# A two-layer graph kernel: the first layer's rows stored in sorted order by SyncE and gathered by the second layer

## The chip, the cores and the metric

The kernel runs on one core of one Trainium2 chip. The metric is the device time of one launch in microseconds (us). Engines are named as the profile names them: PE (TensorE, matmuls; PEld are its weight loads), DVE (VectorE), ACT (ScalarE), POOL (GpSimd) and SP (SyncE, which only issues transfers here).

## What is computed

Sixteen graphs (batches) of 1024 nodes with 64 features are taken through two layers. `adj` is a symmetric 0/1 matrix with the diagonal set.

```python
# layer 0: thin out the neighbours, take weighted quantiles over them per feature, then an MLP
nb      = adj without the diagonal;  m = nb.sum(-1);  rank = cumsum(nb) - 1
skip    = where(m > 10, (m + 1) // 2, 1)
removed = nb & (skip > 1) & ((rank + 1) % skip == 0)        # then symmetrised
valid   = adj with removed and removed.T taken out
agg     = 0.25*q(0.25) + 0.5*q(0.5) + 0.25*q(0.75)          # interpolated quantiles over valid neighbours
y       = relu((x + agg) @ W1 + b1) @ W2 + b2
x1      = layernorm(x + y * nodemask)
# layer 1: messages over the full adjacency
msg     = adj @ x1
d       = tanh(concat(x1, msg) @ W1' + b1') @ W2' + b2'
out     = layernorm(x1 + d)
```

## The kernel before

**Sorting by degree.** For each batch `list_batch` loads the adjacency in eight tiles `a` of 128 rows, makes the neighbour mask `nb` (L623, L626), finds the removed neighbours with matmuls, and counts each node's degree. A counting sort over degrees gives each node its place `at_i` (L685 to L708). Each mask row, with the node's record `mine` (number, degree, the base of the batch's rows in x, nodemask; the constant is set by a GpSimd memset at L681) and its features, is then scattered by GpSimd to its place in the DRAM tensor `order` (L712). From then on, nodes with a similar number of neighbours stand together.

**Groups and chunks.** The sixteen batches form five groups of 2, 4, 4, 4 and 2. The sorted tiles of a group are cut into nine or ten chunks (`CHUNKS`), each with a min/max network of a fixed number of slots, from 40 down to 10. There are 48 chunks. In a chunk by DVE a partition tile mixes rows of all the group's batches; in a chunk by PE (`ChunkByPE`) each tile is of one batch.

**One chunk.** `fetch_lists` loads mask rows (`row`, L806) or features (`x_n`, L931). `fill` of a plain chunk makes neighbour indices with MAX8 (L825 to L831, into `off`, `idx`, with `g.base` added) and gathers neighbours' features slot by slot with GpSimd's indirect DMA (L846, 1012 in all); `fill` of a PE chunk does it with one-hot matmuls (L982, L990). `select` runs the network on DVE (L875), weighs the chosen places (L897, L899), runs the MLP (p_h, p_y) and the layer norm (L550 to L558). At the end of `select` each tile of `y` is scattered by GpSimd to its nodes' rows of the DRAM tensor `g.x1` (L916), so that `g.x1` is in node order. The index of that scatter, `ids`, and the degrees, base and mask of a group in sorted order come from `srt`, which `weigh_group` loads from `order` (L739, L741) before it works out the quantile weights (L744 to L774).

**Second layer.** `messages(g, b)` loads the batch's x1 rows into `x1_n` (L1018; the profile calls it `x_n<-x`; one buffer). Then, eight times, it loads 128 rows of `adj` (L1024), transposes them on PE (L1029), transposes x1 (p_x, L1035), multiplies (p_msg, L1039), and runs the MLP (p_z, tanh L1045, p_d L1048). DVE adds the bias out of p_d into `d` at each of the eight (L1049); p_d has one PSUM buffer, which it shares with p_y. At the end come the residual (L1051), the layer norm and the store (L1053).

**The order of the work.** Each of these is a Python generator. The loop at the end goes through the 48 chunks. Beside the `select` of chunk s it advances, in 24 shares, the `fill` of chunks s+1 and s+2, the `prepare` of the next group (`coming`) and the `finish_group` of the group before (`going`). `prepare` is drained three chunks ahead of its group's first one (`LEAD`). The Tile framework then orders each engine's queue from dependences and its own costs, so an engine's queue isn't exactly in program order. Each engine runs its queue in that order.

Of the kernel before, what the change touches and what calls it, by code (L numbers as in the profile page):

```python
# [9 lines left out]
F32 = mybir.dt.float32  # L10
# [18 lines left out]
INFO = 4  # L29
# [387 lines left out]
def kernel(  # L417
# [37 lines left out]
    off_diag = const.tile([P, P], BF16, name="off_diag")  # L455
    nc.vector.tensor_scalar(off_diag, ident, -1.0, 1.0, op0=ALU.mult, op1=ALU.add)
# [5 lines left out]
    nc.vector.tensor_copy(off_diag_f, off_diag)  # L462
# [22 lines left out]
    zero = const.tile([P, BINS], F32, name="zero")  # L485
    nc.vector.memset(zero, 0.0)
    number = const.tile([P, B * NT], F32, name="number")
    nc.gpsimd.iota(number, pattern=[[P, B * NT]], base=0, channel_multiplier=1,
                   allow_small_or_imprecise_dtypes=True)
# [112 lines left out]
    class Group:  # L602
# [3 lines left out]
        def __init__(self, b0, count):  # L606
            self.b0, self.count, self.tiles, self.run = b0, count, count * NT, P // count
            self.order = [hbm.tile([N, ROW // 2], I32, name=f"order{b0 + i}") for i in range(count)]
            self.x1 = hbm.tile([count * N, C], F32, name=f"x1_{b0}")
            self.parts = []  # L610

    def list_batch(g, b):
# [68 lines left out]
        nc.gpsimd.memset(mine[:, :, 2], float((b + 1) * N))  # L681
        nc.scalar.copy(mine[:, :, 0], number[:, b * NT:(b + 1) * NT])
        nc.scalar.copy(mine[:, :, 3], mask[:, b * NT:(b + 1) * NT])
        deg = mine[:, :, 1]
# [11 lines left out]
        nc.vector.tensor_tensor_scan(base[:, 1:], zero, p[:, :BINS], 0.0, op0=ALU.add, op1=ALU.add)  # L696
# [10 lines left out]
        at_i = work.tile([P, NT], I32, name="at_i")  # L707
# [23 lines left out]
    def weigh_group(g):  # L731
# [11 lines left out]
        ids = work.tile([P, max(GROUPS) * NT], I32, name="ids")[:, :n]  # L743
        nc.vector.tensor_scalar(ids, srt[:, :, 0], float(-g.b0 * N), None, op0=ALU.add)  # L744
        g.local = ids
        g.base, g.mask = srt[:, :, 2], srt[:, :, 3]
        deg = srt[:, :, 1]
# [31 lines left out]
        yield  # L779
# [6 lines left out]
    class Chunk:  # L786
# [26 lines left out]
        def fill(self):  # L813

            g, n = self.g, self.n
            caps = CAPS[g.tiles][self.t0:self.t0 + n]
            wide = -(-(self.k - 1) // 8) * 8
            key = work.tile([P, 96], F16, name="key")[:, :n * wide].rearrange("p (t k) -> p t k", k=wide)
            off = work.tile([P, 96], F32, name="off", bufs=1)[:, :n * wide].rearrange("p (t k) -> p t k", k=wide)
            idx = work.tile([P, 96], I32, name="idx")[:, :n * wide].rearrange("p (t k) -> p t k", k=wide)  # L820
            for t in range(n):
                code = nets.tile([P, N], F16, name="code", bufs=1)
                nc.vector.tensor_mul(code, self.rows[t], down)
                for r in range(0, wide, 8):
                    nc.vector.max(key[:, t, r:r + 8], code)  # L825
                    if r + 8 < wide:
                        nc.vector.match_replace(code, key[:, t, r:r + 8], code, 0.0)  # L827
                yield
            nc.vector.tensor_scalar(off, key, 0.5, OOB, op0=ALU.is_lt, op1=ALU.mult)
            nc.vector.tensor_sub(off, off, key)  # L830
            nc.vector.tensor_add(idx, off, bcast(g.base[:, self.t0:self.t0 + n], wide))  # L831
            self.take_slots()
            at = self.net["slots"]
            for i in range(g.count):
                nc.sync.dma_start(
                    self.a[i * g.run:(i + 1) * g.run, at[0]],
                    g.order[i][self.t0 * g.run:(self.t0 + n) * g.run, XCOL // 2:].bitcast(F32).rearrange(
                        "(t p) c -> p t c", p=g.run))
            for k in range(self.net["low"], self.k):
                nc.scalar.copy(flat(self.a[:, at[k]]),  # L840
                               big[:, (self.k - 1 - k) % 2:(self.k - 1 - k) % 2 + 1].to_broadcast([P, n * C]))
            for k in range(1, max(caps)):
                for t in range(n):
                    if k >= caps[t]:
                        continue
                    nc.gpsimd.indirect_dma_start(  # L846
                        out=self.a[:, at[k], t, :], out_offset=None, in_=x_rows,
                        in_offset=bass.IndirectOffsetOnAxis(ap=idx[:, t, k - 1:k], axis=0),
                        bounds_check=B * N - 1, oob_is_err=False)
                yield  # L850
            self.x_s = self.a[:, at[0]]

        def chosen(self, t, first, count):

            bufs = (self.a.rearrange("p k t c -> p k (t c)"), self.b)
            return [bufs[buf][:, at, t * C:(t + 1) * C]
                    for _, buf, at in self.net["places"][first:first + count]]

# [3 lines left out]
        def select(self):  # L862
# [19 lines left out]
            for h in range(0, n, HT):  # L882
# [23 lines left out]
                p_y = ps_m.tile([P, HT, C], F32, name="p_y", tag="y", bufs=1)  # L906
# [8 lines left out]
            for t in range(n):  # L915
                nc.gpsimd.indirect_dma_start(  # L916
                    out=g.x1, out_offset=bass.IndirectOffsetOnAxis(
                        ap=g.local[:, self.t0 + t:self.t0 + t + 1], axis=0),
                    in_=y[:, t, :], in_offset=None)
            yield  # L920

    class ChunkByPE(Chunk):
# [13 lines left out]
        def fill(self):  # L936
# [8 lines left out]
            for q in range(g.count // 2):  # L945

                degs = work.tile([1, 2, P, 1], F32, name="degs", bufs=1)
                for i in range(2):
                    nc.sync.dma_start(degs[:, i], g.order[2 * q + i][at0:at0 + P, N // 2 + 1:N // 2 + 2].bitcast(
                        F32).rearrange("(o p) i -> o p i", o=1))  # L950
# [53 lines left out]

        def chosen(self, t, first, count):
# [8 lines left out]
    def messages(g, b):  # L1014

        x1 = work.tile([P, NT, C], F32, name="x1_n", bufs=1)
        n0 = (b - g.b0) * N
        nc.sync.dma_start(x1, g.x1[n0:n0 + N, :].rearrange("(t p) c -> p t c", p=P))  # L1018
        d = work.tile([P, NT, C], F32, name="d", bufs=1)
        for h in range(NT // QT):  # L1020
# [25 lines left out]
            p_d = ps_m.tile([P, QT, C], F32, name="p_d", tag="y", bufs=1)  # L1046
            for t in range(QT):
                nc.tensor.matmul(p_d[:, t, :], z_t[:, t * P:(t + 1) * P], w2b_s, start=True, stop=True)  # L1048
            nc.vector.tensor_add(d[:, h * QT:(h + 1) * QT], p_d, b2b_r[:, None, :].to_broadcast([P, QT, C]))  # L1049
            yield  # L1050
        nc.vector.tensor_add(d, d, x1)  # L1051
        layer_norm(work, d, d)
        nc.sync.dma_start(out[b].rearrange("(t p) c -> p t c", p=P), d)  # L1053
        yield

    def prepare(g):
        for b in range(g.b0, g.b0 + g.count):
            yield from list_batch(g, b)
        yield from weigh_group(g)
# [28 lines left out]
    def start(i):  # L1088
        groups[i] = Group(starts[i], GROUPS[i])
        return Side(prepare(groups[i]), GROUPS[i] * (3 * NT + 1) + 1)  # L1090
# [6 lines left out]
    for s in range(-LEAD, len(plan)):  # L1097
# [17 lines left out]
        select = None  # L1115
        if s >= 0:
            i = plan[s][0]
            if s and plan[s - 1][0] != i:
# [41 lines left out]
    work = ctx.enter_context(tc.tile_pool(name="work_g", bufs=1))  # L1160
    ones_row = work.tile([P, N], BF16, name="ones_row")
# [189 lines left out]
```

## Time and profile before

| what | value |
|---|---|
| median of 11 runs | 3148.24 us (3133.44 to 3155.26) |
| the profiled execution | 3143.64 us, span 3141.9 us |
| mean granted PE clock | 0.881 |
| busy: PE / DVE / POOL / ACT | 2383.4 / 2392.6 / 1707.5 / 1574.6 us |
| DMA | 264.34 MB, 84 GB/s over the span |
| x1 scatters (L916) | 128, mean 1429 ns, 350.5 us of POOL idle before them |
| slot gathers (L846) | 1012, mean 1339 ns, 728.2 us of POOL idle before them |
| last layer norm of the first layer (L558 on y) | starts at 3041.8 us |

A row of groups is read as: line, engine, operation, output<-inputs, shape, count, then busy us and mean ns of one, then the engine's idle time just before these instructions and what ended most of it. A row of waits is: engine, tile and line that waited, what it waited for, then total us, number of waits and the longest. In a timeline row the first numbers are the start and the duration in us; in brackets stands the idle time before it with what ended it.

### The profile page before, as it was taken

To read this page: it belongs to the slowest core of one execution; us is meant where nothing else is said; L and a number is where in the kernel's file an instruction comes from. 1 tells how busy PE (TensorE), PEld (TensorE's weight loads), DVE (VectorE), ACT (ScalarE), POOL (GpSimd) and SP (SyncE) were. 2 spreads that over 40 slices of the span, in tenths; PEclk is the share of its full clock that TensorE was granted. 3 is DMA by queue.
4 is the path that set the end of the run, shared out by engine and by line. 5 is a ranking of instruction groups with operands and counts; after the bars stand their busy time and mean duration, and the time that the engine had idled before them with its cause. 6 is when DMAs were issued, how large, how long until landed. Compare 5 with 4: busy or idle time off the path is not lost. (4 is left out here: it accounts for less than half of the span.)

```text
span 3141.9 us, 65767 instructions
## 1 busy us (share of the span) xinstructions
PE 2383.4 (76%) x24920; PEld 1890.8 (60%) x25076; DVE 2392.6 (76%) x5580; ACT 1574.6 (50%) x4045; POOL 1707.5 (54%) x1512
## 2 busy tenths in 40 slices
PE   4456876779586888759888998787889385686977
PEld 2244663457475766547767776666667374575755
DVE  3359985579699978869998888976899387676741
ACT  5624655646254546645566557433554253243543
POOL 3164774256677475757564765485465556333400
PEclk9778987889798998889999999888989697898988
DMA  2520433333222323132334243123222221121222
GB/s 96 158 60 17 120 110 99 98 91 99 82 69 67 123 66 109 50 119 69 114 103 129 62 125 90 50 65 107 73 77 71 69 79 47 51 66 54 82 72 79
DMA packets 221333, 264.34 MB, mean 84 GB/s; under 512 B 147443, under 2 KB 148050, under 8 KB 221008
## 3 DMA queue, kind: packets, MB, share of 16 engines
q1 hardware_dynamic: 174288, 189.31, 19.8%
q0 software_dynamic: 46720, 70.74, 7.8%
q8 instruction: 199, 3.26, 0.4%
q14 instruction: 126, 1.03, 0.1%
HBM read 218.20 MB, written 46.40 MB: 84 GB/s over the span
## 5 line engine op out<-in xcount | busy, mean ns | idle before, releaser
L846 POOL DMA_INDIRECT slots_a<-in_x_dram,idx x1012 | 1355.1, 1339 | 728.2 <-issue 266.0
L990 PE MATMUL p_slots<-hot,parts 128*64 128x256 bf16 (+1 forms) x12288 | 695.1, 269 | 141.0 <-DVE hot L982 136.2
L990 PEld LDWEIGHTS <-parts 128*64 128x64 bf16 x12288 | 632.5, 113 | 179.4 <-issue 111.8
L875 DVE TENSOR_TENSOR slots_b<-slots_a 128x256 f32<-128x256 f32 (+14 forms) x582 | 359.3, 633 | 92.7 <-DMA slots_a<-in_x_dram,idx 58.6
L916 POOL DMA_INDIRECT x<-y,ids x128 | 182.9, 1429 | 350.5 <-DVE y L558 210.3
L899 PE MATMUL p_g<-ident,terms 128*64 128x128 f32 x1988 | 281.6, 295 | 62.5 <-ACT terms L897 61.8
L982 DVE TENSOR_SCALAR hot<-val 128x2048 bf16<-128x2048 bf16 x456 | 310.9, 702 | 15.6 <-PE p_slots L990 12.4
L899 PEld LDWEIGHTS p_g<-ident,terms 128*64 128x64 f32 x1988 | 240.5, 149 | 95.2 <-ACT terms L897 77.8
L875 DVE TENSOR_TENSOR slots_a<-slots_b 128x256 f32<-128x256 f32 (+11 forms) x526 | 288.6, 561 | 0.6
L1039 PE MATMUL p_msg<-adj_t,x_n 128*64 128x128 f32 x2048 | 272.1, 286 | 7.9 <-ACT adj_t L1030 4.2
L1039 PEld LDWEIGHTS p_msg<-adj_t,x_n 128*64 128x64 f32 x2048 | 232.9, 143 | 31.3 <-issue 9.8
L630 ACT ACTIVATE gone<-nb 128x512 bf16<-128x512 bf16 x256 | 159.8, 627 | 174.3 <-DVE nb L626 173.1
L1001 ACT COPY slots_a<-p_slots 128x512 f32<-128x512 f32 (+2 forms) x136 | 72.9, 536 | 300.5 <-PE p_slots L990 243.6
L660 PE MATMUL p_rank<-reach,nb_t 128*128 128x128 bf16 (+3 forms) x956 | 177.0, 318 | 58.4 <-ACT nb_t L654 49.0
L1029 PE MATMUL p_adj<-ident,a 128*128 128x128 f32 x1024 | 185.0, 294 | 43.2 <-ACT adj_t L1030 21.6
L662 ACT ACTIVATE gone<-p_rank,s 128x512 bf16<-128x512 f32 x256 | 166.4, 684 | 97.5 <-PE p_rank L660 84.6
L825 DVE MAX8 key<-code 128x8 f16<-128x1024 f16 x170 | 207.9, 1223 | 2.0 <-DVE code L827 0.5
L712 POOL DMA_INDIRECT order<-nb,at_i x128 | 145.8, 1139 | 110.0 <-issue 40.3
L875 DVE TENSOR_TENSOR slots_b<-slots_b 128x256 f32<-128x256 f32 (+11 forms) x310 | 199.3, 643 | 0.4
L660 PEld LDWEIGHTS <-nb_t 128*128 128x128 bf16 x1024 | 96.8, 105 | 164.8 <-ACT nb_t L654 78.7
L1030 ACT COPY adj_t<-p_adj 128x512 f32<-128x512 f32 x256 | 149.2, 583 | 74.0 <-PE p_adj L1029 72.0
L1049 DVE TENSOR_TENSOR d<-p_d,b2b_r 128x64 f32<-128x64 f32 x128 | 28.5, 223 | 204.3 <-PE p_d L1048 203.2
(189 smaller groups left out, 4607.8 us busy)
## 6 DMA issues: line engine op xcount, KB each, us to landing
a<-in_adj_dram SPq DMA_DIRECT2D x256, 512.0 KB
row_p<-order SPq DMA_DIRECT2D x64, 256.0 KB
slots_a<-in_x_dram,idx POOLq DMA_INDIRECT x1012
row<-order SPq DMA_DIRECT2D x192, 64.0 KB
nb<-in_x_dram SPq DMA_DIRECT2D x128, 32.0 KB
row<-order SPq DMA_DIRECT2D x32, 128.0 KB
x_s<-in_x_dram SPq DMA_DIRECT2D x16, 256.0 KB
x_n<-x SPq DMA_DIRECT2D x16, 256.0 KB
```

Of the source, the lines that this page charges most:

```text
L630: nc.scalar.activation(r[:, cols], nb[:, cols], AF.Copy, accum_out=m[:, h, t - half_b * HT:t - half_b * HT + 1])
L660: nc.tensor.matmul(p[:, c * P:], nb_t[:, (h * HT + c) * P:(h * HT + c + 1) * P], reach[:, :HALF - c * P], start=False, stop=c == HT - 1)
L662: nc.scalar.activation(r[:, h * HALF:(h + 1) * HALF], p, AF.Abs, bias=biases[h][:, col], scale=2.0)
L825: nc.vector.max(key[:, t, r:r + 8], code)
L846: nc.gpsimd.indirect_dma_start(out=self.a[:, at[k], t, :], out_offset=None, in_=x_rows, in_offset=bass.IndirectOffsetOnAxis(ap=idx[:, t, k ...
L875: nc.vector.tensor_tensor(view(rb, ra, [(d[0], d[1 + side]) for d in dims]), view(ab, aa, [(d[0], d[1]) for d in dims]), view(bb, ba, [(d[ ...
L899: nc.tensor.matmul(p[:C, col], terms[:, i], ident, start=False, stop=t == e - 1 and first + i == places - 1)
L916: nc.gpsimd.indirect_dma_start(out=g.x1, out_offset=bass.IndirectOffsetOnAxis(ap=g.local[:, self.t0 + t:self.t0 + t + 1], axis=0), in_=y[: ...
L982: nc.vector.tensor_scalar(hot[:, :, :, e], val, float(inside[at]), None, op0=ALU.is_equal)
L990: nc.tensor.matmul(p[i * C:(i + 1) * C, o:o + w], g.parts[2 * q + i][:, c, h], hot[:, c, i, :w], start=c == 0 and h == 0, stop=c == NT - 1 ...
L1029: nc.tensor.transpose(p[:, j, :], a[:, col:col + P], ident)
L1039: nc.tensor.matmul(p[C:2 * C, :QUART], x1[:, j, :], adj_t[:, j, :], start=(j == 0), stop=(j == NT - 1))
```

## The change

The x1 rows of the first layer are no longer put into node order by scatters. SP stores each chunk's `y` in sorted order, with plain transfers, into one DRAM tensor per batch (`keep`); `messages` gathers a batch's rows into node order with eight indirect DMAs on GpSimd, by the places of the counting sort, which are now kept for all batches (`places`). The node number and the base leave the record `mine`; the base is a constant per group. `weigh_group` is no longer a step of `prepare`: it is called one chunk ahead of its group's first `select`. The messages of a group start one chunk later. p_d takes all eight quarters of a batch in one bank and is read once; p_y moves to tag "m". `x1_n` has two buffers and `idx` three. Some constants go.

```diff
-INFO = 4
+INFO = 2
...
-            self.x1 = hbm.tile([count * N, C], F32, name=f"x1_{b0}")
+            self.x1 = [hbm.tile([N, C], F32, name=f"x1_{b0 + i}") for i in range(count)]
+            self.base = const.tile([P, 1], F32, name=f"base_{b0}")
+            for i in range(count):
+                nc.gpsimd.memset(self.base[i * self.run:(i + 1) * self.run], float((b0 + i + 1) * N))
...
         mine = work.tile([P, NT, INFO], F32, name="mine")
-        nc.gpsimd.memset(mine[:, :, 2], float((b + 1) * N))
-        nc.scalar.copy(mine[:, :, 0], number[:, b * NT:(b + 1) * NT])
-        nc.scalar.copy(mine[:, :, 3], mask[:, b * NT:(b + 1) * NT])
-        deg = mine[:, :, 1]
+        nc.scalar.copy(mine[:, :, 1], mask[:, b * NT:(b + 1) * NT])
+        deg = mine[:, :, 0]
...
-        at_i = work.tile([P, NT], I32, name="at_i")
+        at_i = places[:, b * NT:(b + 1) * NT]
...
-        ids = work.tile([P, max(GROUPS) * NT], I32, name="ids")[:, :n]
-        nc.vector.tensor_scalar(ids, srt[:, :, 0], float(-g.b0 * N), None, op0=ALU.add)
-        g.local = ids
-        g.base, g.mask = srt[:, :, 2], srt[:, :, 3]
-        deg = srt[:, :, 1]
+        g.mask = srt[:, :, 1]
+        deg = srt[:, :, 0]
...
-            idx = work.tile([P, 96], I32, name="idx")[:, :n * wide].rearrange("p (t k) -> p t k", k=wide)
+            idx = work.tile([P, 96], I32, name="idx", bufs=3)[:, :n * wide].rearrange("p (t k) -> p t k", k=wide)
...
-            nc.vector.tensor_sub(off, off, key)
-            nc.vector.tensor_add(idx, off, bcast(g.base[:, self.t0:self.t0 + n], wide))
+            nc.vector.scalar_tensor_tensor(idx, off, g.base, key, op0=ALU.add, op1=ALU.subtract)
...
+        def keep(self, y):          # in Chunk
+            g = self.g
+            for i in range(g.count):
+                nc.sync.dma_start(
+                    g.x1[i][self.t0 * g.run:(self.t0 + self.n) * g.run].rearrange("(t p) c -> p t c", p=g.run),
+                    y[i * g.run:(i + 1) * g.run])
...
-                p_y = ps_m.tile([P, HT, C], F32, name="p_y", tag="y", bufs=1)
+                p_y = ps_m.tile([P, HT, C], F32, name="p_y", tag="m")
...
-            for t in range(n):
-                nc.gpsimd.indirect_dma_start(
-                    out=g.x1, out_offset=bass.IndirectOffsetOnAxis(
-                        ap=g.local[:, self.t0 + t:self.t0 + t + 1], axis=0),
-                    in_=y[:, t, :], in_offset=None)
+            self.keep(y)
...
+        def keep(self, y):          # in ChunkByPE
+            at = slice(self.t0 * self.g.run, self.t0 * self.g.run + P)
+            for i in range(self.n):
+                nc.sync.dma_start(self.g.x1[i][at], y[:, i])
...
-        x1 = work.tile([P, NT, C], F32, name="x1_n", bufs=1)
-        n0 = (b - g.b0) * N
-        nc.sync.dma_start(x1, g.x1[n0:n0 + N, :].rearrange("(t p) c -> p t c", p=P))
-        d = work.tile([P, NT, C], F32, name="d", bufs=1)
+        x1 = work.tile([P, NT, C], F32, name="x1_n")
+        for t in range(NT):
+            nc.gpsimd.indirect_dma_start(
+                out=x1[:, t], out_offset=None, in_=g.x1[b - g.b0],
+                in_offset=bass.IndirectOffsetOnAxis(ap=places[:, b * NT + t:b * NT + t + 1], axis=0))
+        p_d = ps_m.tile([P, NT, C], F32, name="p_d", tag="y", bufs=1)
...
-            p_d = ps_m.tile([P, QT, C], F32, name="p_d", tag="y", bufs=1)
             for t in range(QT):
-                nc.tensor.matmul(p_d[:, t, :], z_t[:, t * P:(t + 1) * P], w2b_s, start=True, stop=True)
-            nc.vector.tensor_add(d[:, h * QT:(h + 1) * QT], p_d, b2b_r[:, None, :].to_broadcast([P, QT, C]))
+                nc.tensor.matmul(p_d[:, h * QT + t, :], z_t[:, t * P:(t + 1) * P], w2b_s, start=True, stop=True)
             yield
-        nc.vector.tensor_add(d, d, x1)
-        layer_norm(work, d, d)
+        nc.vector.tensor_add(x1, x1, b2b_r[:, None, :].to_broadcast([P, NT, C]))
+        nc.vector.tensor_add(x1, x1, p_d)
+        layer_norm(work, x1, x1)
...
     def prepare(g):
         for b in range(g.b0, g.b0 + g.count):
             yield from list_batch(g, b)
-        yield from weigh_group(g)
...
+        if s + 1 < len(plan) and (s < 0 or plan[s][0] != plan[s + 1][0]) and s + 1 >= 0:
+            weigh_group(groups[plan[s + 1][0]])
         if s >= 0:
             i = plan[s][0]
-            if s and plan[s - 1][0] != i:
+            if s > 1 and plan[s - 1][0] == i != plan[s - 2][0] and i:
```

## The prediction

> **What bounds the kernel now.** I read the busy line first, then the waits of VectorE (DVE) and TensorE (PE), then the timelines of both over one another. The second and third columns of a wait are its total in us and its count, the last its longest.
>
> ```profile
> span 3141.9 us, 65767 instructions
> PE 2383.4 (76%) x24920; PEld 1890.8 (60%) x25076; DVE 2392.6 (76%) x5580; ACT 1574.6 (50%) x4045; POOL 1707.5 (54%) x1512
> ```
>
> No engine is full: DVE and PE both stand for some 750 us. The waits say behind what.
>
> ```profile
> POOL x L916 <- DVE y L558: 210.3, 11, 53.1
> DVE d L1049 <- PE p_d L1048: 203.2, 59, 25.9
> ...
> DVE nb L626 <- DMA order<-nb,at_i: 91.3, 30, 26.9
> ...
> PE p_x L1035 <- DMA x_n<-x: 78.5, 9, 22.9
> ...
> POOL x L916 <- DMA x<-y,ids: 74.6, 38, 3.9
> ...
> DVE slots_b L875 <- DMA slots_a<-in_x_dram,idx: 58.6, 5, 30.1
> ...
> DVE ids L744 <- DMA srt<-order: 52.5, 4, 45.7
> ...
> DVE idx L831 <- DMA slots_a<-in_x_dram,idx: 38.6, 2, 24.2
> ```
>
> Five of the DVE and PE rows end in a DMA that GpSimd (POOL) issues, or that SyncE (SP) may issue only after one of POOL's: the `order` scatter, the x1 scatter (`x<-y`), the gather of slots. The first row shows why POOL is late: eleven times it stood, up to 53.1 us, at an x1 scatter whose layer norm had not run, with gathers queued behind.
>
> A wait costs time where the other engine has nothing either. An example from DVE's timeline, and PE's at another place:
>
> ```profile
> 2448.17 1.22 DVE L825 MAX8 key<-code 128x8 f16<-128x1024 f16 x1
> 2495.10 0.18 DVE L744 TENSOR_SCALAR ids<-srt 128x16 int32<-128x16 f32 x1 [45.72 <-DMA srt<-order]
> ```
>
> ```profile
> 2697.67 0.49 PE L968 MATMUL p_nth<-val,ones_h 128*128 128x256 bf16 x3
> 2720.55 0.42 PE L1035 MATMUL p_x<-ident,x_n 128*64 128x128 f32 x1 [22.39 <-DMA x_n<-x]
> 2720.90 3.67 PE L1039 MATMUL p_msg<-adj_t,x_n 128*64 128x128 f32 x16
> ```
>
> Laying both engines over one another, I kept the stretches over 3 us after 300 us in which neither runs. By what ended them: `order` scatter 23.3 (at 816) + 12.5 (2127) = 35.8; x_n load 17.6 (1392) + 9.8 (2039) + 18.6 (2702) + 6.3 (3042) = 52.3; srt load 41.1 (2454); gathers 4.4 (485) + 6.4 (666) + 11.6 (2640) + 15.9 (2830) = 38.3. Left out: a 3.6 at 518, and 3.2 after the last norm. Together **167.5 us**, all behind POOL's queue.
>
> **What the Trainium skill says.** "PSUM — Partial Sum Buffer", section "Engine vs sequencer instructions": the queues of ScalarE, VectorE and GpSimd are strict FIFO. The trace agrees: at 2716 POOL stands 53.1 us at a scatter and issues no gather. "DMA: Bandwidth & Descriptors", section "Anatomy of one DMA — SWDGE (gpsimd) path": a DMA's wait is kept by the issuing sequencer, not by the DMA engine; so SP too stops at a store whose data isn't there. SP's own waits agree (105.9 us at the x_n load, L1018, for scatters). The same section puts a fixed 2 us on one DMA; here 38 scatters that waited for an earlier one waited 74.6 / 38 = 1.96 us. "TensorE: Matmul & The Clock Gate", section "What's actually happening": PE drops to half clock after an idle window of about 3.4 us. The trace agrees: the same 16 p_msg took 1.96 us at 3064 and 3.67 after the 22.39 us above. So a closed hole gives back a little more than its length; I don't count that.
>
> **The change, part by part.**
>
> *Scatter to store and gather.* Out: 128 x1 scatters (1429 ns, 182.9 us of POOL) with 350.5 us of idle before them. In: 128 gathers of x1 rows, 8 ahead of each batch; nearest row the slot gather, 1339 ns, so 171 us. POOL's busy time is a wash; the places differ. In the built order POOL meets x1 in 16 clumps, not after every chunk, and each clump waits for stores one chunk older. The 16 memsets of `mine` also leave, but their 147.2 us of waiting is the wait of the scatter next in line, for the same `nb`: nothing. Credit against the 167.5: `order` scatters and x_n 60% each (21 + 31), since 84 slot gathers still stand ahead of some clumps; gathers and idx 70% (27; idx gets a third buffer, and its index no longer waits for srt). Ends: nothing to all.
>
> *weigh_group late.* L744 goes, and the rest stands one or two layer norms later in DVE's order. Cover: over a chunk of some 60 us between load and use. 90% of 41.1: 37. If the cover is gone the wait comes back whole.
>
> *p_d gathered in one bank.* 128 adds of 223 ns (28.5 us) become 16 of some 686 (11.0, the row of L1051). With `ids` and one op less per index list DVE loses about 18 us; half on the path: 9. More: DVE no longer stands at p_d every quarter. 203.2 us of that wait, less 74.2 in the last 100 us, where DVE has nothing else, less 46.0 counted above (x_n at 1392, 2039, 2702), leaves 83 in which PE worked. I take a quarter, 21 (ends 0 and 83).
>
> *Start.* For the second batch nine srt loads stand ahead of the row loads on SP, from 143.10 to 148.47; they move behind: 5.
>
> *Tail.* The messages of a group start one chunk later. The last p_y is followed by 21 quarters of messages in the built order, 16 before. A quarter takes 4.38 us alone (p_msg at 3064.05 and 3068.43): +22. Those five cover the first gather (PE waited 9.8 at 3042, of which 6.3 is counted above), and the second x_n buffer takes the 3.1 us wait at 3090 with its half-clock run: -8. Sum +14.
>
> *SP.* 156 stores in, 16 loads out; an issue takes 0.3 to 0.6 us, some 60 us of SP's time, which has room. New: SP stops at each of 48 chunks until the layer norm is done; behind stand loads of `a`, rows and slots, for which DVE and PE wait. Nearest: SP already waits 96.0 us in 13 for y at L931, 7.4 each, and DVE waits for `a` only 18 us between 610 and 2420. I take +15; ends 0 and +60.
>
> *Nothing:* halved srt records, constants, `off` as bf16, p_y under tag m: too small, or off the path; p_y now shares two banks with p_g, which could cost a few us.
>
> Sum: -21 -31 -27 -37 -9 -21 -5 +14 +15 = **-122**. The profiled execution took 3143.6 us with a span of 3141.9, 4.6 below the median of 3148.2; against the median: 3026.
>
> **The rivals.**
>
> *POOL's backlog stays.* The gathers stand behind slot gathers (84 x (1.34 + 0.3) = 138 us of issue ahead of batch 10's), so PE's x_n wait only changes its name. For: POOL issued without pause from 2400 to 2486. Against: three waits (28.6, 22.0, 12.5) had just made it late. Then 21, 31 and 27 go: -43, about 3105.
>
> *All of it goes.* Every hole (167.5), half of the 83, and DVE's 18: -167 -42 -18 -5 +14 = -218, about 2930.
>
> *SP becomes the wall: slower.* Stores that wait for the layer norm hold back the next loads of `a` (three buffers for two users). Place: SP's queue, at the end of each chunk. Its price is 48 times the exposed part of one wait. The gains without SP are 137, so it decides from 2.9 us a chunk; at the 7.4 of L931, fully exposed, 355 - 137 = +218, near 3366; at 3.5, +31. Against: SP waits 413 us for buffers at L1024 in the body today with little harm.
>
> *It doesn't do what it says:* excluded for the scatters, which are gone from the built order; late waits could remain as x_n clumps that wait for their buffer (the first rival).
>
> **How the numbers follow.** A difference of 0.2%, about 6 us, is what can be told from none. Forecast (2975 to 3070) 0.45; backlog stays (3070 to 3135) 0.25; all goes (2920 to 2975) 0.18; SP wall 0.12, of which 0.09 is slower and 0.03 within 0.2%. Predicted 3026; range 2940 to 3135. Faster 0.88, same 0.03, slower 0.09.
>
> **What would show it.** Right: no DVE wait on srt over 5 us; `d`'s wait for p_d outside the tail gone; DVE's wait on `order` below 50; PE's on x_n below 40; POOL's waits at L916 not replaced by more than 100 at the x1 gather; tail after the last y 110 to 125 us. Wrong: DVE or PE waiting for `a`, rows or slots by over 60 us more (SP), or x_n waits of 20 us still there (backlog).

## The result and the profile after

The changed kernel takes 3112.75 us (median; 3110.2 to 3121.44) where the kernel before takes 3147.95 beside it: a ratio of 0.9895, 95% interval 0.9876 to 0.9914, about 33 us less. The forecast was 122 less. The direction is right and the time lies in the stated range; the gain is about a quarter of the forecast.

The page of the changed kernel, its span and busy line. The profiled execution before had a span of 3141.9.

```profile
span 3114.3 us, 65701 instructions
PE 2389.5 (77%) x24918; PEld 1886.4 (61%) x25076; DVE 2386.8 (77%) x5434; ACT 1593.4 (51%) x4047; POOL 1770.8 (57%) x1511
```

PE and DVE are busy as long as before, within 6 us each; ACT has 19 us more, POOL 63. So the change was one of waits. The waits of the changed kernel (us in all, times, longest):

```profile
POOL order L708 <- issue: 303.2, 88, 51.7
...
DVE nb L624 <- DMA order<-nb,places: 139.2, 34, 30.2
...
DVE ln_st L549 <- ACT ln_sq L548: 105.2, 33, 24.6
...
POOL x_n L1017 <- DMA x<-y: 86.2, 2, 69.9
...
DVE a L621 <- DMA a<-in_adj_dram: 72.2, 32, 15.8
...
DVE x_n L1050 <- PE p_msg L1040: 71.1, 3, 28.3
...
PE p_x L1036 <- DMA x_n<-x,places: 22.2, 2, 15.7
```

Gone are DVE's waits for srt (52.5 before), for p_d (203.2) and, nearly, PE's for x_n (78.5). DVE's wait for the `order` scatter did not fall with them: 91.3 became 139.2. And the layer norm's wait for ACT's square grew from 36.6 to 105.2, the wait for `a` from 49.7 to 72.2. In the kernel before:

```profile
DVE a L623 <- DMA a<-in_adj_dram: 49.7, 28, 5.7
...
DVE ln_st L555 <- ACT ln_sq L554: 36.6, 21, 5.7
```

A stretch in which neither DVE nor PE runs is called a hole here. With the two timelines laid over one another as in the prediction, the holes over 3 us after 300 us are now: `order` scatter 29.8 (at 411) + 3.7 + 18.0 (828) + 8.1 (1499) + 21.0 (2148) = 80.6; gathers 9.6; x_n 3.6; srt 0; the load of `a` 11.6 (2192); x_s 3.4. Before, they were 39.4 for `order` (counted alike: with the 3.6 at 518 that the prediction left out of its 35.8), 52.3 for x_n, 41.1 for srt and 38.3 for gathers. The holes of srt, x_n and gathers nearly closed, and the `order` holes doubled.

The largest of them, at 411 us, opens before the first row of x1 is gathered (724 us). The change also takes one step out of the count that paces a group's lists (L1090 before, L1089 now), because `weigh_group` is no longer a step of `prepare`. With it batch 3's `order` scatter moved from behind 95 slot gathers to behind 124. The prediction has no term for this. A hole of 29.0 us stands at 411 in the late weights alone too (below), where x1 is still scattered, and none stands there with the count raised again (p1_pace).

Over the whole span the time in which neither runs fell from 294.3 to 244.2 us, 50.1 less. The span fell by only 27.6, because the time in which both run at once fell as well, from 1928.4 to 1906.2 us. PE's and DVE's busy times together changed by 0.3 us; with the same work to do, a microsecond of overlap that is lost costs as much as one of a hole.

POOL's rows show where its idle time went. Groups of the kernel before (busy, mean ns, then idle before them):

```profile
L846 POOL DMA_INDIRECT slots_a<-in_x_dram,idx x1012 | 1355.1, 1339 | 728.2 <-issue 266.0 <-ACT slots_a L840 128.7 <-PE p_chosen L1011 49.0
L916 POOL DMA_INDIRECT x<-y,ids x128 | 182.9, 1429 | 350.5 <-DVE y L558 210.3 <-DMA x<-y,ids 74.6 <-DVE idx L831 28.6
L712 POOL DMA_INDIRECT order<-nb,at_i x128 | 145.8, 1139 | 110.0 <-issue 40.3 <-DVE at_i L708 32.5 <-ACT slots_a L1001 16.7
...
L681 POOL MEMSET mine<- 128x8 f32 x16 | 3.2, 207 | 147.2 <-DVE nb L711 147.2
```

and of the changed kernel:

```profile
L837 POOL DMA_INDIRECT slots_a<-in_x_dram,idx x1012 | 1425.3, 1408 | 787.8 <-issue 267.5 <-ACT slots_a L831 156.0 <-PE p_msg L1040 76.3
L708 POOL DMA_INDIRECT order<-nb,places x128 | 166.4, 1300 | 318.7 <-issue 303.2 <-ACT gone L628 3.7 <-DVE places L704 3.6
L1017 POOL DMA_INDIRECT x_n<-x,places x128 | 155.6, 1215 | 166.4 <-DMA x<-y 86.2 <-issue 29.9 <-DVE slots_b L873 24.7
```

Ahead of these groups POOL's idle time was 728.2 + 350.5 + 110.0 + 147.2 = 1335.9 us before; now it is 787.8 + 318.7 + 166.4 = 1272.9. The 147.2 at the memsets only moved to the scatter behind them, as the prediction said: ahead of both it was 257.2, and it is 318.7. Of the 350.5 at the x1 scatters, 166.4 stand at the x1 gathers now, 61.5 more at the `order` scatters and 59.6 more at the slot gathers. The profile names nothing for the 303.2 at the `order` scatters ("issue"), but each of the twelve waits over 3 us there ends 0.3 to 0.9 us after DVE wrote `places` (L704), the scatter's index. This sum is close to the span less POOL's busy time, so it had to stay large while the span did; it tells where POOL stands, not why.

### The profile page after: what moved, and what is told of

Same layout as the page of the kernel before. It is cut to its first block, busy times and chain, and to the rows that moved or that the text cites. A ratio compares the mean times of both kernels' runs of the same rounds, so it can differ in the third digit from the quotient of the medians.

```text
span 3114.3 us, 65701 instructions
## 1 busy us (share of the span) xinstructions
PE 2389.5 (77%) x24918; PEld 1886.4 (61%) x25076; DVE 2386.8 (77%) x5434; ACT 1593.4 (51%) x4047; POOL 1770.8 (57%) x1511
## 5 line engine op out<-in xcount | busy, mean ns | idle before, releaser
L837 POOL DMA_INDIRECT slots_a<-in_x_dram,idx x1012 | 1425.3, 1408 | 787.8 <-issue 267.5
L984 PE MATMUL p_slots<-hot,parts 128*64 128x256 bf16 (+1 forms) x12288 | 713.3, 271 | 198.5 <-DVE hot L976 170.3
L984 PEld LDWEIGHTS <-parts 128*64 128x64 bf16 x12288 | 639.0, 114 | 242.0 <-issue 112.0
L708 POOL DMA_INDIRECT order<-nb,places x128 | 166.4, 1300 | 318.7 <-issue 303.2
L1040 PE MATMUL p_msg<-adj_t,x_n 128*64 128x128 f32 x2048 | 283.5, 291 | 36.3 <-ACT adj_t L1031 15.9
L1040 PEld LDWEIGHTS p_msg<-adj_t,x_n 128*64 128x64 f32 x2048 | 237.7, 145 | 67.9 <-DMA x_n<-x,places 19.1
L1017 POOL DMA_INDIRECT x_n<-x,places x128 | 155.6, 1215 | 166.4 <-DMA x<-y 86.2
L1030 PE MATMUL p_adj<-ident,a 128*128 128x128 f32 x1024 | 186.2, 297 | 47.3 <-DMA a<-in_adj_dram 24.2
L658 PE MATMUL p_rank<-reach,nb_t 128*128 128x128 bf16 (+3 forms) x957 | 169.6, 309 | 66.6 <-ACT nb_t L652 58.0
L624 DVE TENSOR_SCALAR nb<-a 128x1024 bf16<-128x1024 f32 x128 | 89.5, 701 | 139.8 <-DMA order<-nb,places 139.2
```

Source lines behind the costliest of these rows:

```text
L658: nc.tensor.matmul(p[:, c * P:], nb_t[:, (h * HT + c) * P:(h * HT + c + 1) * P], reach[:, :HALF - c * P], start=False, stop=c == HT - 1)
L708: move = nc.gpsimd.indirect_dma_start(out=g.order[b - g.b0], out_offset=bass.IndirectOffsetOnAxis(ap=at_i[:, t:t + 1], axis=0), in_=nbs[t] ...
L837: nc.gpsimd.indirect_dma_start(out=self.a[:, at[k], t, :], out_offset=None, in_=x_rows, in_offset=bass.IndirectOffsetOnAxis(ap=idx[:, t, k ...
L984: nc.tensor.matmul(p[i * C:(i + 1) * C, o:o + w], g.parts[2 * q + i][:, c, h], hot[:, c, i, :w], start=c == 0 and h == 0, stop=c == NT - 1 ...
L1030: nc.tensor.transpose(p[:, j, :], a[:, col:col + P], ident)
L1040: nc.tensor.matmul(p[C:2 * C, :QUART], x1[:, j, :], adj_t[:, j, :], start=(j == 0), stop=(j == NT - 1))
```

## What took the place of the holes

POOL at 2156 to 2170 us in the changed kernel, and DVE at the end of its longest wait there:

```profile
2155.01 1.00 POOL L837 DMA_INDIRECT slots_a<-in_x_dram,idx  x1 [0.30 <-issue]
2156.32 0.95 POOL L1017 DMA_INDIRECT x_n<-x,places  x1 [0.30 <-issue]
...
2165.09 0.94 POOL L1017 DMA_INDIRECT x_n<-x,places  x1 [0.30 <-DMA x_n<-x,places]
2166.34 1.01 POOL L708 DMA_INDIRECT order<-nb,places  x1 [0.30 <-DMA x_n<-x,places]
```

```profile
2169.26 0.69 DVE L624 TENSOR_SCALAR nb<-a 128x1024 bf16<-128x1024 f32 x1 [27.12 <-DMA order<-nb,places]
```

DVE needs a free `nb` tile for the next batch (there are nine), and only the `order` scatter of the batch before frees one. The last of batch 14's rows was written at 2132 and its `places` at 2138. POOL, which had been issuing slot gathers without a pause since 2117, then issued 13 more and eight x1 gathers (10 us), and reached the scatter at 2166. The clump of x1 gathers stands directly ahead of the `order` scatter at batches 7, 11 and 14 (scatters at 843, 1504 and 2166); at batches 13 and 15 too, but there the scatter then waited 6.3 and 3.6 us for its own rows. The clump isn't the whole of it: in the late weights alone, with no x1 gather, the hole at this scatter is 22.2 us long (at 2112): there 23 slot gathers and one x1 scatter stood between `at_i` (2099) and the scatter (2131).

The second new wait runs through three engines at 1441 us. POOL first, then PE, ACT and DVE:

```profile
1442.24 0.96 POOL L1017 DMA_INDIRECT x_n<-x,places  x1 [0.31 <-issue]
```

```profile
1444.61 0.42 PE L1036 MATMUL p_x<-ident,x_n 128*64 128x128 f32 x1 [15.74 <-DMA x_n<-x,places]
```

```profile
1445.07 0.26 ACT L1037 COPY node_t<-p_x 64x128 f32<-64x128 f32 x1 [15.02 <-PE p_x L1036]
```

```profile
1465.61 0.22 DVE L549 TENSOR_REDUCE ln_st<-ln_sq 128x1 f32<-128x64 f32 x1 [24.56 <-ACT ln_sq L548]
```

The x1 gathers stood behind 33 slot gathers. PE waited at p_x, ACT in its own order at the copy behind it, and the square of a layer norm that has nothing to do with this batch was queued behind that copy and the ones after it; DVE stood 24.56 us for it. The Trainium skill, "PSUM — Partial Sum Buffer", section "Engine vs sequencer instructions", calls these queues strict FIFO; this chain shows it on three of them at once.

## The experiments

Eight of the runs (x1 to x4, h1 to h4) fell on two chips on which the kernel before took 3851 to 3866 us and these eight versions 3880 to 3953, with 206 to 354 us in which PE stood at p_slots for nothing that the profile shows (0.7 in the kernel before above). They are told at the end and decide nothing on the other chips. All the rest ran on three chips where the kernel before took 3132 to 3136, so that 1% is 31 us. A ratio is a version's time over that of the kernel before, measured beside it on the same chip.

**The late weights alone** (p3_weigh). In the kernel before:

```diff
-        g.base, g.mask = srt[:, :, 2], srt[:, :, 3]
+        g.mask = srt[:, :, 3]          # g.base: a constant per group
...
-        yield from weigh_group(g)      # end of prepare; now called a chunk ahead of the group's first select
-        return Side(prepare(groups[i]), GROUPS[i] * (3 * NT + 1) + 1)
+        return Side(prepare(groups[i]), GROUPS[i] * (3 * NT + 1))
```

The index of a slot gather takes one DVE operation less, since the base is a constant, and the constant `zero` went, to make room. Expected:

> The kernel before with only the weights of a group worked out late, the constant base, and the step taken out of the list count, on another chip. As predicted: the srt wait goes, 37 to 42 us less, ratio 0.987-0.988. Theory A: a hole of 20 to 30 us opens near 411 us, since batch 3's order scatter stands behind 123 slot gathers, not 95; of the 41 only 10 to 20 us are left, ratio 0.993-0.997.

Measured: 0.9846 (0.9821 to 0.9872), 48 us less: more than either theory allowed, and more than the whole change gains. The span and two waits of its profile:

```profile
span 3090.6 us, 65912 instructions
```

```profile
POOL x L915 <- DVE y L556: 313.6, 11, 57.8
```

```profile
DVE nb L627 <- DMA order<-nb,at_i: 143.5, 33, 29.0
```

The srt wait is gone and so is DVE's wait at idx (38.6). POOL still stands 313.6 us at x1 scatters, more than the 210.3 before, and yet this is the fastest kernel of these that computes everything: the length of POOL's standing doesn't by itself decide the time. The hole of 29.0 at 411 did open as theory A said, and did not cost what A said. Of the 41.1 us of the srt hole, 14.1 came back as a wait for rows of `order` (at 2469).

**The p_d part alone** (g2_pd). In the kernel before:

```diff
-        d = work.tile([P, NT, C], F32, name="d", bufs=1)
+        p_d = ps_m.tile([P, NT, C], F32, name="p_d", tag="y", bufs=1)   # all quarters; read once at the end
...
-        x1 = work.tile([P, NT, C], F32, name="x1_n", bufs=1)
+        x1 = work.tile([P, NT, C], F32, name="x1_n")
...
-                p_y = ps_m.tile([P, HT, C], F32, name="p_y", tag="y", bufs=1)
+                p_y = ps_m.tile([P, HT, C], F32, name="p_y", tag="m")
```

> The kernel before with only the p_d part: all quarters in one PSUM bank, d dropped, x1_n with two buffers, p_y under tag m. As predicted: 25 us less (9 of adds, 21 of the wait, less a few), ratio 0.990-0.993. Rival G (the wait for p_d was slack; VectorE reaches its next wait sooner): the p_d wait of 203 us goes, others grow, ratio 0.997-1.005.

Measured: 1.0114 (1.0067 to 1.0160), 36 us more. From DVE's waits:

```profile
DVE nb L626 <- DMA order<-nb,at_i: 109.6, 32, 21.5
DVE idx L831 <- DMA slots_a<-in_x_dram,idx: 78.7, 3, 31.4
DVE x_n L1049 <- PE p_msg L1039: 73.3, 6, 41.0
```

The 203.2 us at p_d are gone, but DVE's waits in all rose from 736 to 784: 73.3 for p_msg in their place, idx 38.6 to 78.7, `hot` for PE 12.4 to 39.4, `order` 91.3 to 109.6. The time came out above both expected ranges: rival G is right that other waits grow, and had them too small. The prediction's step had priced the wait's end and not what comes next.

**p_y's tag alone** (k2_py): only the last pair of lines of the diff above.

> The kernel before with only p_y moved to the two banks of tag m. Theory (p_y's sharing with p_g, p_x, p_msg and p_z made the p_d part cost 1.1%): ratio 1.007-1.013. Rival (the cost lies in p_d held for a whole batch, or in the order of the work that follows from it): ratio 0.997-1.003.

Measured: 1.0021 (0.9998 to 1.0044), as the rival said. The shared banks alone are not what made the part dear; whether p_d held for a whole batch or the shifted order did is open.

**The p_d part undone in the changed kernel** (k1_nopd):

```diff
-        p_d = ps_m.tile([P, NT, C], F32, name="p_d", tag="y", bufs=1)
+        d = work.tile([P, NT, C], BF16, name="d", bufs=1)
...                                      # p_d by quarters again, p_y in tag "y" again
```

> The changed kernel with the p_d part undone (p_d and the add to d for each quarter, p_y in its own bank, d in bf16 so that two x1_n buffers still fit). If the p_d part costs here what it cost alone (+1.1%): ratio 0.976-0.981, and order waits of VectorE shrink or stay. Rival (here it saves VectorE the adds and waits, as predicted): 0.997-1.001. If the parts just don't add: 0.985-0.992.

Measured: 0.9937 (0.9917 to 0.9956). Here the part is worth 0.9895 - 0.9937 = -0.0042, some 13 us, of gain (with d in bf16 on the other side of the comparison). The ratio lies just above the range given for parts that don't add, and well outside the two others: the parts don't add. Its largest wait of DVE:

```profile
DVE nb L624 <- DMA order<-nb,places: 175.1, 28, 38.3
```

Put together:

| kernel | ratio | us against before | `order` holes | neither runs | both run |
|---|---|---|---|---|---|
| before | 1 | 0 | 39.4 | 294.3 | 1928.4 |
| late weights | 0.9846 (0.9821 to 0.9872) | -48 | 76.5 | 255.6 | 1954.4 |
| late weights, x1 stored and gathered | 0.9937 (0.9917 to 0.9956) | -20 | 122.7 | 252.6 | 1944.1 |
| late weights, x1 stored and gathered, p_d (the change) | 0.9895 (0.9876 to 0.9914) | -33 | 80.6 | 244.2 | 1906.2 |
| p_d alone | 1.0114 (1.0067 to 1.0160) | +36 | 54.5 | 306.3 | 1898.5 |

The last three columns (us) are of one profiled execution each; "neither" and "both" are PE and DVE. The change has the fewest microseconds in which neither runs, and yet the late weights alone are faster: they gained 26 us of overlap where the change lost 22.

The step from late weights to the next row, with the move that gives the change its name, costs 0.9% or 28 us; the intervals don't touch. The two rows were measured on different chips of the three, and the step holds more than the move: messages begun a chunk later, a second x1_n and a third idx buffer, d in bf16. By the layer norms of the two profiles, from the 19th chunk to the 31st the late weights alone took 819 us, with x1 gathered 854; from there to the last norm 805 against 772; and the tail after it 102.2 against 112.1. In all these two executions lie only 17 us apart, so where the 28 arise is not settled.

**The pace of the lists** (p1_pace). In the changed kernel the count of steps is raised by four, which brings batch 3's `order` scatter back behind 95 slot gathers:

```diff
-        return Side(prepare(groups[i]), GROUPS[i] * (3 * NT + 1))
+        return Side(prepare(groups[i]), GROUPS[i] * (3 * NT + 1) + 4)
```

> The pace test on another chip. Theory A: batch 3's order scatter is back behind 95 slot gathers, the 29.8 us hole at 411 us goes, DVE's wait for the order scatter falls from 139 to about 110 us, and the time falls by 20 to 30 us, to 0.980-0.983 of the kernel before. Rival B: the head start is lost in the middle groups, the ratio stays at 0.988-0.991.

Measured: 1.0206 (1.0172 to 1.0241), slower than both kernels. Theory A fell. The hole at 411 went and the seventh chunk's norm came at 584 us, not 612; but a hole of 42.2 opened at 787, and 24.0, 31.8 and 34.4 later:

```profile
DVE nb L624 <- DMA order<-nb,places: 197.4, 28, 43.5
```

```profile
PE p_adj L1030 <- DMA a<-in_adj_dram: 99.1, 6, 54.6
```

DVE asked for `nb` sooner; from batch 10 on POOL's scatters came no sooner. What DVE wins ahead of POOL it waits for at the next `order` scatter. SP, in order, stood up to 81.5 us at the load into the same `nb` (from about 2133 to 2214) and issued the `a` for PE only then (2228): PE's wait for `a`, 24.2 in the changed kernel, became 99.1.

**A pause after each scatter** (g4_pause): four empty steps in `list_batch` after the scatters, with the count raised by as many.

```diff
-        yield
+        for _ in range(5):
+            yield
...
-        return Side(prepare(groups[i]), GROUPS[i] * (3 * NT + 1))
+        return Side(prepare(groups[i]), GROUPS[i] * (3 * NT + 1 + 4))
```

> The changed kernel with four empty steps after each batch's order scatter, so that VectorE's next nb tiles stand later in its order while the scatters keep their places in POOL's queue (batch 3's is back behind 99 slot gathers, not 124). Theory A: a step is about 5.5 us (640 us of a group over 116 steps), so up to 22 us of slack at each batch: VectorE's wait for the order scatter falls from 139 to below 70 us, the holes of 80 us to below 30, ratio 0.970-0.982. Rival B: the work that is moved only makes other waits, as the faster pace did: ratio 0.986-1.0.

Measured: 1.0195 (1.0160 to 1.0229). DVE's wait at `nb` fell to 117.0, and one stretch of 77.7 us with neither engine opened at 2127:

```profile
PE p_y L907 <- ACT h_t L904: 83.9, 8, 80.4
...
ACT gone L628 <- DVE nb L624: 277.9, 57, 80.6
...
DVE a L621 <- issue: 80.8, 1, 80.8
...
SPq L623 <- DMA order<-nb,places: 483.3, 86, 86.4
```

Read from the bottom, this is the `order` scatter again. SP stood 86.4 us at the load into `nb`, which only batch 14's scatter frees: its `places` were written at 2111, but POOL issued slot and x1 gathers until 2189. The next `a` stood behind that load in SP's queue and was issued at 2199.6; DVE waited for this `a`, ACT in its order for DVE's `nb`, and PE for ACT's h_t. The wait didn't shrink; it moved from the row of `nb` to that of `a`. Theory A missed again, and rival B's reading holds at a higher price than its range.

**The x1 gathers earlier** (g1_ahead):

```diff
+            with tc.high_priority(offset=2000):
                 nc.gpsimd.indirect_dma_start(
                     out=x1[:, t], out_offset=None, in_=g.x1[b - g.b0], ...
```

> The changed kernel with the x1 gathers given priority, which moves batch 6's from behind 454 slot gathers in POOL's queue to behind 441 (about 20 us earlier), batch 3's from 206 to 173 and the others by 0 to 12 places; nothing else moves by design. Theory E (the late gathers stop TensorE at p_x, ScalarE behind it and through the layer norm VectorE, the three long waits of 24.6, 11.9 and 11.7 us for ln_sq): TensorE's waits for x_n (22 us at p_x, 12 at p_msg) and those three go, the time falls by 15 to 35 us, ratio 0.978-0.985. Rival F (SP standing at the stores delays a and costs the time): the ratio stays within 0.003 of 0.9895.

Measured: 0.9892 (0.9861 to 0.9923), the changed kernel's ratio. PE's wait at p_x is gone and the ln_sq wait fell from 105.2 to 76.1 (longest 10.9, 24.6 in the changed kernel); the `order` wait grew from 139.2 to:

```profile
DVE nb L624 <- DMA order<-nb,places: 165.4, 31, 42.4
```

So the chain through these engines is real, and breaking it gained nothing that could be told from the change: DVE reached the same late scatter earlier and waited there (`order` holes 110.1, against 80.6). F fits the ratio, but the trace gives another reason than F's.

**Stores that wait for no layer norm** (p4_sp). SP stores the loaded rows `x_s` in place of `y`; the true first-layer rows are left out.

```diff
-                    y[i * g.run:(i + 1) * g.run])
+                    self.x_s[i * g.run:(i + 1) * g.run])
...
-                nc.sync.dma_start(self.g.x1[i][at], y[:, i])
+                nc.sync.dma_start(self.g.x1[i][at], self.x_s[:, i])
```

> The changed kernel, but SP stores the loaded x rows (x_s) in place of y, so that no store waits for a layer norm; the true first-layer rows are left out. As predicted (SP standing at the stores costs 15 us, at most 60): SP's waits for y (207 us in all) and DVE's wait for a (72 us, 50 before) fall, ratio 0.974-0.985. Rival (SP's waits are covered by its lead): the waits for y go, DVE's waits change by less than 15 us, and the ratio stays at 0.988-0.991.

Measured: 0.9787 (0.9759 to 0.9815), 34 us below the changed kernel, inside the range expected but not by the way expected. Of the 207 us of SP's waits for y, 125.6 stood at stores and went; the rest stands at a load (L925: 81.9, now 67.9). DVE's wait for `a` stayed (72.2 before this edit):

```profile
DVE a L621 <- DMA a<-in_adj_dram: 70.4, 28, 16.1
DVE ln_st L549 <- ACT ln_sq L548: 63.7, 33, 4.8
```

The predicted way, late loads of `a`, is not how SP's stores cost. With the stores free, the built order also put the first x1 gathers of a group some 220 us earlier (1215 against 1442), so the 34 us are what stores and gathers together cost by depending on a layer norm, in this order of work; the run doesn't part them.

**Messages begun at the group's first chunk** (p2_early):

```diff
-            if s > 1 and plan[s - 1][0] == i != plan[s - 2][0] and i:
+            if s and plan[s - 1][0] != i:
```

> Messages begun at the next group's first chunk, on another chip. Theory C (the later start costs time): the tail falls by about 20 us and the ratio to 0.974-0.983. Rival D (the gathers of x1 then stand in POOL at stores that wait for a layer norm): POOL waits over 100 us more at the x1 gather, TensorE's wait for x_n is above 60 us, and the ratio rises to 0.992-1.002.

Measured: 0.9878 (0.9855 to 0.9901), not to be told from the change. The tail fell from 109.4 to 103.3, by 6 us and not by C's 20. PE's wait at p_x rose from 22.2 to 48.4 (with 15.0 at p_msg 63.4, as D said), but the ratio didn't rise.

**Ten `nb` buffers for one of x1_n** (g3_nb10):

```diff
-                nb = held.tile([P, ROW], BF16, name="nb")
+                nb = held.tile([P, ROW], BF16, name="nb", bufs=NT + 2)
...
-        x1 = work.tile([P, NT, C], F32, name="x1_n")
+        x1 = work.tile([P, NT, C], F32, name="x1_n", bufs=1)
```

> The changed kernel with ten nb buffers, not nine, paid for by one x1_n buffer, not two. Theory A (VectorE waits at nb for a buffer that only the order scatter frees, and POOL's queue decides when): one buffer more lets the wait begin one list step later, 5 to 6 us at each of 16 batches, and of the 80 us of holes some 40 go: ratio 0.975-0.983, less up to 5 us for the lost x1_n buffer. Rival B (closed holes come back as other waits): ratio within 0.003 of 0.9895.

Measured: 1.0693 (1.0655 to 1.0731). The `order` wait fell to 97.7, as A says, but the price was misjudged:

```profile
PE p_x L1036 <- DMA x_n<-x,places: 249.8, 11, 62.9
```

```profile
POOL x_n L1017 <- DMA out_dram<-x_n: 138.1, 4, 60.0
```

With one buffer POOL stands at the x1 gather until the batch ahead has been stored, and everything queued behind it stands too. The trace puts the loss to the missing buffer. With d in f32 two x1_n buffers need the room that the p_d part frees, but with d in bf16 they fit without it (k1_nopd). The run with one x1_n buffer and nothing else (h1_x1one) fell on one of the two other chips, and there PE waited only 35.3 us at p_x, though POOL stood 167.3 us at the x1 gather for the batch ahead. So this stays argued from one trace, and that the tenth `nb` buffer did part of the harm isn't excluded.

**On the two other chips.** x1_pace, x2_early, x3_pd, x4_weigh and h2_nopd, h3_pace, h4_py carry the edits shown above (h3_pace takes only the extra step out of the count, in the kernel before); h1_x1one is the second line pair of g3's diff.

> The changed kernel with one number altered: the count of steps by which a group's lists are paced is 4 higher, so that batch 3's order scatter stands behind 95 slot gathers in POOL's queue, as in the kernel before, and not behind 124. Theory A (the place of the order scatter in POOL's queue, moved by the pace, opened the 29.8 us hole at 411 us): the hole at 411 goes, DVE's wait for the order scatter falls from 139 to about 110 us, and the time falls by 20 to 30 us, to 3083-3093. Rival B (the head start is lost anyway in the middle groups): the hole goes, but the time stays within 6 us of 3113.

Measured 1.0027 (1.0000 to 1.0053).

> The changed kernel with the messages of a group begun at the next group's first chunk, as in the kernel before, not at its second. Theory C (beginning one chunk later costs time, in the tail by five more quarters and in the middle groups, which took 54 us longer than before): the tail after the last norm falls by about 20 us, and the time by 20 to 50 us, to 3063-3093. Rival D (the gathers of x1 would then meet stores that wait for a layer norm, with slot gathers queued behind them in POOL): POOL waits over 100 us more at the x1 gather, TensorE's wait for x_n returns above 60 us, and the time rises by 10 to 40 us, to 3123-3153.

Measured 1.0243 (1.0207 to 1.0279).

> The kernel before with only the p_d part: all quarters in one PSUM bank, d dropped, x1_n with two buffers, p_y under tag m. As predicted (adds that leave VectorE, its wait for p_d gone): about 25 us less, 3123. Rival (VectorE's wait for p_d only changes its name to the next late thing): the p_d wait of 203 us goes, but the time changes by less than 10 us.

Measured 1.0060 (1.0037 to 1.0084).

> The kernel before with only the weights of a group worked out late, the constant base, and the step taken out of the list count. As predicted: the wait for srt goes and the time falls by 37 to 42 us, to about 3106-3111. Theory A: the missing step moves batch 3's order scatter from behind 95 slot gathers to behind 123, a hole of 20 to 30 us opens near 411 us, and of the 41 only 10 to 20 us are left: 3128-3138.

Measured 1.0059 (1.0037 to 1.0082).

> The changed kernel with one x1_n buffer in place of two, nothing else. Theory H (the gather of x1 by POOL can't be issued before the batch ahead has left x1_n, and then stands in POOL behind whatever was queued: the second buffer, paid for by dropping d, is what makes the gather bearable): TensorE's wait at p_x for x_n rises from 22 to above 150 us and the ratio to 1.04-1.08, as in the run with ten nb buffers. Rival (it was the tenth nb buffer that did the harm): ratio within 0.005 of 0.9895.

Measured 1.0243 (1.0188 to 1.0298).

> The changed kernel with the p_d part undone: p_d and the add to d for each quarter, p_y in its own bank again; d in bf16, so that two x1_n buffers still fit. If the p_d part costs here what it cost alone (+1.1%): ratio 0.976-0.981. Rival (with two x1_n buffers and no late weights the part saves VectorE the adds and the waits, as predicted, 30 us): 0.997-1.001. If neither: 0.987-0.992.

Measured 1.0221 (1.0156 to 1.0286).

> The kernel before with only the pace of the lists changed: the step count of a group without the extra one, as in the changed kernel; the weights stay where they are. Theory (the pace made part of the late weights' 48 us): faster by 10 to 30 us, ratio 0.990-0.997, although batch 3's order scatter moves from behind 95 slot gathers to behind 121. Rival (the place of the scatter is all that the pace does, the hole of 29 us at 411 us opens and costs): ratio 1.003-1.010.

Measured 1.0103 (1.0069 to 1.0137).

> The kernel before with only p_y moved to the two banks of tag m. Theory (p_y's sharing with p_g, p_x, p_msg and p_z is what made the p_d part cost 1.1%): ratio 1.007-1.013. Rival (the cost lies in p_d held for a whole batch, or in the order of the work): ratio 0.997-1.003.

Measured 1.0091 (1.0062 to 1.0121).

A wait of PE of such a run (x3_pd):

```profile
PE p_slots L990 <- issue: 265.6, 305, 2.5
```

The p_d part alone and the late weights alone come out level here (1.0060 and 1.0059); on the other chips they lie 2.7% apart (1.0114 and 0.9846). Raising the count (x1_pace, 1.0027) gave here the lowest ratio of the four variants of the changed kernel, and on the other chips one of the highest. The changed kernel itself was not measured here; its four variants took as long as the kernel before or up to 2.4% more. So neither its gain nor that of the late weights is shown for these two chips. How much of the late weights' 48 us is the missing step of the pace (h3_pace) is therefore open.

## Why the prediction was right or wrong

The forecast's direction was right, its size was not. The step that failed is the sum: it took each closed hole as time won, with overlap left as it was, and let the `order` holes shrink with POOL's standing at x1 scatters. By its steps:

- **`order` scatter holes, -21:** the wrong sign. 39.4 became 80.6, +41. The step took the lateness of the scatters for POOL's standing at x1 scatters, and let it shrink with that. 29.8 of the 80.6 come from the pace of the lists, which the prediction put at nothing without naming it. For the rest, POOL reaches the scatters late behind slot gathers and, at three of them, behind a clump of x1 gathers (10 us), which were counted as a wash; but with x1 still scattered (the late weights alone) these holes are 76.5 too.
- **x_n holes, -31, and gathers, -27:** as holes right (52.3 to 3.6, 38.3 to 9.6), more than forecast. As time they were not all gain: g1_ahead took the rest of PE's wait for x_n and won nothing.
- **srt, -37, and the start, -5:** as hole and as start right: the srt hole is gone, and the first layer norm comes at 290, not 297. The late weights alone gave 48; how much of that is the srt wait, the constant base or the pace is open.
- **p_d, -9 and -21:** wrong. +36 alone, about -13 within the change. A wait that ends for an in-order engine is not time won until it is known what is late next; the quarter that the prediction took of the 83 us had no such reason. DVE's busy time fell by 6 us, not by 18.
- **Tail, +14:** right in sign, a little large: the tail went from 99.9 to 109.4, +9.5.
- **SP, +15:** the waits at the stores are there, but not shown to cost that much. DVE's wait for `a`, the predicted way, grew by 22 us, and stayed when the stores waited for nothing (p4_sp); stores and gathers together cost 34 us there. The larger of the two waits at the stores (the other, at L1002, is 25.4):

```profile
SPq L853 <- DVE y L552: 100.2, 18, 39.4
```

As a sum: closing 119 us of holes brought 41 of `order` and 15 of other holes over 3 us, 12 of other time in which neither runs, and 22 us less of overlap. Of the rivals, "POOL's backlog stays" (3105, 43 less) came nearest to the 33 measured. Its mechanism, late work in POOL's queue whose waits only change their name, is in the trace at the `order` scatters; at x_n, where it put it, the waits fell. That its sum fits is luck: it kept the terms of p_d (-30) and srt (-37), where the runs gave about -13 and, with the parts that go with it, -48. "SP becomes the wall" did not happen: DVE's wait for `a` grew by 22 us and PE's by 7, not by 60.

Of the marks, srt, p_d, x_n (22.2 + 11.7 at p_msg) and POOL's waits for stores at the x1 gather (86.2; 166.4 for all it waited there) came out as for "right", the tail nearly (109.4 against 110 to 125); DVE's wait on `order` (139.2 against below 50) is the one that told.

The version that beats both kernels is the late weights alone, by ratios taken on different chips; on one of the two other chips it took 0.6% longer than the kernel before.

## What to carry to other kernels

Where two in-order engines wait for one another through a third one's queue, a hole that is closed upstream can open at the next place where that queue is late; before adding holes up, follow the fast engine to its next wait on the same queue. The name of a wait can hide this: here the same late scatter showed as a wait for `nb`, for `a`, or for ACT. Count the overlap of the two busiest engines beside the holes, since both make up the time. And test the parts of a change one by one: here one part gave more than the whole, and one cost time alone and gained some in company.

## What the runs showed of the hardware

Chips differ by more than most changes: the kernel before took 3132 to 3136 us on three chips and 3851 to 3866 on two, with a granted clock of 0.88 to 0.89 there and 0.80 to 0.82 here. In the eight versions run on these two, PE stood 206 to 354 us at p_slots with no wait that the profile names (0.7 in the kernel before above). One issue of an `order` scatter took 11.93 us (at 2173.49) between others of 1.0 to 3.0, with no wait shown; that row's mean is 1300 ns, 1139 before.
